# Sums of exponentials in the last chunk of an image attention: adds by VectorE and GpSimd in place of products with ones

## The chip, the cores and the metric

One core of one Trainium2 chip runs the whole program. The time is device microseconds of one execution; before the change the median of three runs is 12066.05 us (12055.0 to 12073.83). A matrix product runs on TensorE (PE in the profile), elementwise work on VectorE (DVE), ScalarE (ACT) and GpSimd (POOL). Each engine works through its own list of instructions in order; semaphores tie the lists together.

## The reference, cut to what matters

Four images of 56 x 56 points with 128 channels go through four layers. The first and the last layer are the same block: a window attention, then an attention over the whole image, then an MLP. The change lies in the attention over the whole image, so it is executed eight times (two layers, four images):

```python
def _mha(x, wq, bq, wk, bk, wv, bv, wo, bo):      # x: one image, 3136 points x 128 channels, 4 heads of 32
    ...
    scores = jnp.einsum('nhqd,nhkd->nhqk', q, k) / jnp.sqrt(jnp.float32(dk))
    attn = jax.nn.softmax(scores, axis=-1)
    out = jnp.einsum('nhqk,nhkd->nhqd', attn, v)
    ...
xf = xf + _mha(_layernorm(xf, g1, be1), wq, bq, wk, bk, wv, bv, wo, bo)
```

The softmax divides by the sum of exponentials over all 3136 keys. That sum, one number for each query and head, is what the change computes in another way.

## The kernel before

**Tiling.** The 3136 queries are cut into NCK = 7 chunks of CH = 448, the keys into NKB = 25 blocks of 128 (the last has 64). One step g of the loop (from L611) is one chunk and one block: qc is the chunk, k the block, g = 25 qc + k. Scores are made transposed, keys on the partitions and queries along the row, so a sum over keys runs partly over blocks (an add of whole tiles) and partly over the 128 partitions (a product with ones).

**One step on TensorE.** For each of four heads, `shifted` (L543) puts minus the row maximum into a PSUM bank, `score` (L552) adds keys times queries; ScalarE then writes the exponentials (L553) into a tile `e` that holds two heads, 128 x 896. `p = 0` is the pair of heads 0 and 1, `p = 1` heads 2 and 3; in an even step pair 0 comes first, in an odd step pair 1. At the end of the step `values(g - 1)` (L579) multiplies the values with the exponentials of the step before and gathers in the bank `po` over the whole chunk. PSUM banks of the tag "mm" go round in a ring of 7 (L500), tiles `e` in a ring of 12 (L551), that is six steps.

**The sum over the keys** has two ways. In `summed` (L555 to L563) GpSimd adds the tile `e` of block k onto a running tile `es`, one instruction for each pair of heads. Where k is in `by_ones(qc)` (L538) that add is left out, and `values` instead multiplies four heads by a matrix of ones into a bank `pd` (L568, called at L582), which ScalarE copies to `rest` the first time (L585) and VectorE adds to it afterwards (L587). In chunks 0 to 5 the blocks 4, 8, ... 24 go by ones (6 of 25), in the last chunk the blocks 4, 6, ... 24 (11 of 25). When a chunk is over, `total` (L594) multiplies `es` by ones into the bank `pt` (L568 too) and VectorE adds `rest` (L597); ScalarE inverts it by a logarithm and an exponential (`invert`, L602 and L604), GpSimd multiplies (L608).

**Order around it.** All is emitted in the order of the loop, by hand. `total(qc - 1)` comes at the end of step k = 4 of the next chunk, the two halves of `invert(qc - 1)` at the start of steps 5 and 6, ahead of the exponentials of these steps on ScalarE. The last chunk has no next one: its `total`, `invert` and product follow directly after its last `values`. Then the MLP begins, whose banks take the PSUM space of the loop (first product L683).

**Other work in the loop.** While chunks 0 to 5 run, TensorE and VectorE also find the row maxima of later queries (L371, L376). In the last chunk no maxima are left.

Of the kernel before, what the change touches and what calls it, by code (L numbers as in the profile page):

```python
# [10 lines left out]
F32 = mybir.dt.float32  # L11
# [3 lines left out]
ALU = mybir.AluOpType  # L15
# [4 lines left out]
P = 128  # L20
HW = 56
L = HW * HW
CH = 448
NCK = L // CH
# [10 lines left out]
NKB = (L + KB - 1) // KB  # L35
# [43 lines left out]
class _Net:  # L79
# [249 lines left out]
    def attention(self, layer, b, x1, oT, sb):  # L329
# [9 lines left out]
        nc, tc, w, x = self.nc, self.tc, self.w[layer], self.x_of(b)  # L339
# [23 lines left out]
        with tc.manual_schedule():  # L363
# [134 lines left out]
            with tc.tile_pool(name="at_sb", bufs=2) as tb, tc.tile_pool(name="at_ps", bufs=2, space=PSUM) as ps:  # L498
# [36 lines left out]

                made, es, sums = {}, {}, {}

                by_ones = lambda qc: range(4, NKB, 4) if qc < NCK - 1 else range(4, NKB, 2)  # L538
                pst = {}

                def shifted(g, h):
# [13 lines left out]
                def summed(g, p):  # L555
                    qc, k = divmod(g, NKB)
                    nk = min(KB, L - k * KB)
                    if k == 0:
                        if qc not in sums:
                            sums[qc] = tb.tile([P, NH, CH], F32, tag="es", name="es")  # L560
                    elif k not in by_ones(qc):
                        s = sums[qc][:nk, 2 * p : 2 * p + 2, :]
                        nc.gpsimd.tensor_tensor(s, es[g - 1, p][:nk] if k == 1 else s, es[g, p][:nk], ALU.add)  # L563

                def ones(n, src, into):

                    for h in range(NH):
                        nc.tensor.matmul(into[head(h), :CH], lhsT=self.one32[:n], rhs=src(h)[:n], start=True, stop=True)  # L568
# [25 lines left out]
                def total(qc):  # L594
                    pd = bank("pt")
                    ones(P, lambda h: sums[qc][:, h, :], pd)
                    nc.vector.tensor_add(made[qc]["rest"], pd[:, :CH], made[qc]["rest"])  # L597

                def invert(qc, step):
                    r = made[qc]["rest"]  # L600
# [10 lines left out]
                for g in range(ng + 8):  # L611
                    qc, k = divmod(g, NKB)
# [4 lines left out]
                    p = g % 2  # L617
# [4 lines left out]
                    if g < ng:  # L622


                        maxima(early_max, True)
                        maxima(late_max, False)
                        for h in first:
                            shifted(g, h)
                        for h in first:
                            score(g, h)  # L630
                        summed(g, p)
                    if g < ng:
                        shifted(g, early_max)
                        score(g, early_max)
                        shifted(g, late_max)
                        maxima(first[0], False)
                        score(g, late_max)
                        maxima(first[1], False)
                        summed(g, 1 - p)
# [3 lines left out]
                    if qc >= 1 and k == 4:  # L643
                        total(qc - 1)
# [991 lines left out]
```

## Time and profile before

The profiled execution took 12079.11 us, with a span of 12077.3 us from its first to its last instruction; the median of the runs is 12066.05 us. A table of what matters here, from the page and from windows of the trace:

| | first six chunks, first attention | last chunk, first attention | whole span |
|---|---|---|---|
| stretch, us from the start | 191.7 to 670.2 | 670.2 to 733.9 | 0 to 12077.3 |
| length, us | 478.5 | 63.7 | 12077.3 |
| TensorE busy, us | 476.7 | 63.1 | 10924.2 |
| VectorE busy, us | 368.8 | 8.1 | 9398.6 |
| ScalarE busy, us | 294.1 | 48.6 | 7556.4 |
| GpSimd busy, us | 450.7 | 55.1 | 9397.2 |

A busy TensorE is not one at its peak: its products are pipelined and up to four small ones run side by side, so their own durations add up to more than the busy time. In a group's line of the profile stand the source line, the engine, the operation, its output and inputs with their shapes, the count, the busy time, the mean length of one instruction in ns, and then the idle time of the engine just before these instructions with what ended it. In a timeline the first two numbers are the start in us and the length in us of a run of equal instructions.

### The profile page before, as it was taken

The page shows a single profiled execution, that of the slowest core. Times are in us where ns is not written, and L with a number is a line of the kernel's source. Part 1 is how long each engine was busy: PE and PEld are TensorE (multiplying, and loading weights), DVE is VectorE, ACT ScalarE, POOL GpSimd, SP SyncE. Part 2 cuts the span into 40 slices and gives each one's busy share as a digit, 9 for nine tenths or more (in the row PEclk, how much of TensorE's full clock was granted, in tenths as well). Part 3 has the DMA queues.
Part 4 walks back from the last instruction along what each step waited for, and adds up shares of the span by engine and source line. Part 5 has one row for each costly group of instructions (what it writes and reads, how often), then busy time and mean ns, then how long its engine had stood idle before and what let it go on. Part 6 is the DMA issues. An engine that isn't in the chain of part 4 may idle for free.

```text
span 12077.3 us, 219818 instructions
## 1 busy us (share of the span) xinstructions
PE 10924.2 (90%) x86844; PEld 7150.1 (59%) x86844; DVE 9398.6 (78%) x12051; ACT 7556.4 (63%) x19327; POOL 9397.2 (78%) x5876
## 2 busy tenths in 40 slices
PE   8998998997899899999889989999988998997799
PEld 5538885544688755454468865545446886553454
DVE  6749996767999877475899977747589997775674
ACT  5677776564677656656467765665646776564366
POOL 4949995795799759488689975948868997596497
PEclk9999999998899999999989999999989999998899
DMA  1000000005100000000610000000051000004200
GB/s 66 2 14 6 5 5 1 1 1 169 54 6 5 2 1 1 12 1 5 175 45 5 5 2 1 2 12 1 13 174 38 5 5 2 1 1 143 69 2 7
DMA packets 146295, 321.10 MB, mean 27 GB/s; under 512 B 17980, under 2 KB 87664, under 8 KB 145136
## 3 DMA queue, kind: packets, MB, share of 16 engines
q0 software_dynamic: 70848, 231.27, 6.6%
q1 hardware_dynamic: 74128, 74.57, 2.0%
q8 instruction: 687, 11.26, 0.4%
q14 instruction: 344, 2.82, 0.1%
q10 hardware_dynamic: 288, 1.19, 0.0%
HBM read 259.05 MB, written 47.90 MB: 25 GB/s over the span
## 4 chain that ended last, share of the span: by engine, by line
PE 59%; DVE 16%; POOL 11%; ACT 9%; issue 4%; DMA 1%; DVEq 0%; POOLq 0%; ACTq 0%; SPq 0%
PE pm L371 15%; PE po L579 10%; DVE hs L1126 9%; POOL hs L1135 9%; PE pst L552 7%; PE pst L543 3%; PE pd L568 2%; PE yt L1144 2%; PE pyb L1165 2%; PE dbu L1108 2%; PE pvt L1460 2%; DVE dgb L1012 1%; PE pdo L1468 1%; DVE mx L376 1%; ACT da L1063 1%
## 5 line engine op out<-in xcount | busy, mean ns | idle before, releaser
L376 DVE TENSOR_REDUCE mx<-pm 128x1 f32<-128x512 f32 (+7 forms) x6424 | 3377.5, 560 | 999.9 <-PE pm L371 924.1
L563 POOL TENSOR_TENSOR es<-es,e 128x896 f32<-128x896 f32 x1824 | 3764.1, 2090 | 77.1 <-ACT e L553 29.1
L1126 DVE TENSOR_TENSOR_SCAN hs<-da,dbu 128x928 f32<-128x928 f32 x1792 | 3617.4, 2068 | 31.9 <-ACT dbu L1119 16.1
L553 ACT ACTIVATE e<-pst 128x448 f32<-128x448 f32 (+1 forms) x5600 | 2592.0, 548 | 1530.3 <-PE pst L552 1076.3
L1135 POOL TENSOR_TENSOR hs<-hs,cb 128x896 f32<-128x896 f32 x1792 | 3434.8, 1950 | 16.4 <-ACT carry L1130 14.5
L371 PE MATMUL pm<-ks,qs 32*128 32x448 f32 (+5 forms) x12848 | 2963.9, 528 | 13.4 <-DVE nm L397 7.8
L552 PE MATMUL pst<-qs,ks 32*128 32x448 f32 x11200 | 2324.2, 539 | 0.0
L371 PEld LDWEIGHTS pm<-ks,qs 32*128 32x128 f32 x12848 | 1281.3, 187 | 1119.3 <-DVE mx L376 621.6
L1144 PE MATMUL yt<-w_C,hs 128*116 128x128 f32 x14336 | 1877.6, 274 | 16.2 <-POOL hs L1135 14.3
L543 PE MATMUL pst<-nm,sel 32*128 32x448 f32 x5600 | 1666.4, 527 | 6.9 <-DVE nm L397 6.9
L1144 PEld LDWEIGHTS yt<-w_C,hs 128*116 128x116 f32 x14336 | 1567.8, 136 | 42.2 <-POOL hs L1135 31.8
L1108 PE MATMUL dbu<-dgb,ut 112*128 112x224 f32 x7168 | 1248.7, 296 | 202.3 <-DVE hs L1126 199.4
L579 PE MATMUL po<-e,va 128*32 128x448 f32 (+1 forms) x11200 | 1358.6, 554 | 0.0
L1335 POOL DMA_INDIRECT g<-tab,idx x900 | 870.2, 967 | 505.9 <-issue 203.8
L552 PEld LDWEIGHTS pst<-qs,ks 32*128 32x128 f32 x11200 | 1253.9, 187 | 1.4
L1063 ACT ACTIVATE da<-dl,A 128x112 f32<-128x112 f32 x3584 | 1193.9, 382 | 0.1
L1108 PEld LDWEIGHTS dbu<-dgb,ut 112*128 112x128 f32 x7168 | 946.5, 192 | 323.4 <-DVE hs L1126 311.4
L543 PEld LDWEIGHTS pst<-nm,sel 32*128 32x128 f32 x5600 | 710.5, 185 | 164.3 <-issue 145.5
L1130 ACT COPY carry<-hs 128x32 f32<-128x32 f32 x1792 | 396.3, 221 | 551.0 <-DVE hs L1126 530.6
L297 POOL TENSOR_TENSOR pz<-s,m 64x784 f32<-64x784 f32 x128 | 191.8, 1498 | 681.2 <-DVE m L294 676.7
L579 PEld LDWEIGHTS po<-e,va 128*32 128x32 f32 (+1 forms) x11200 | 222.5, 108 | 824.8 <-issue 762.8
L1080 PE MATMUL pt<-w_C,dh 128*112 128x128 f32 x3584 | 551.7, 278 | 152.4 <-DVE dgb L1012 146.2
(227 smaller groups left out, 14365.6 us busy)
## 6 DMA issues: line engine op xcount, KB each, us to landing
g<-tab,idx POOLq DMA_INDIRECT x900, 3.7
tab<-zero SPq DMA_DIRECT2D x4, 3364.0 KB
dl_d<-dl SPq DMA_DIRECT2D x28, 448.0 KB
dl<-dl_d SPq DMA_DIRECT2D x56, 224.0 KB
tab<-gt SPq DMA_DIRECT2D x16, 448.0 KB
out_dram<-x SPq DMA_DIRECT2D x28, 224.0 KB
tab<-gt SPq DMA_DIRECT2D x16, 336.0 KB
x<-in_x_dram SPq DMA_DIRECT2D x21, 224.0 KB
```

The source lines that it names most:

```text
L371: nc.tensor.matmul(pm[:, at : at + m], lhsT=qs[head(h), q : q + P], rhs=ks[head(h), keys], start=True, stop=True)
L376: nc.vector.tensor_reduce(mx[:, i, h, n : n + 1], p, AX.X, ALU.max)
L543: nc.tensor.matmul(pst[g, h][:, :CH], lhsT=self.sel[head(h), :], rhs=nm[head(h), part(g // NKB)], start=True, stop=False)
L552: nc.tensor.matmul(t[:, :CH], lhsT=ks[head(h), k * KB : (k + 1) * KB], rhs=qs[head(h), part(qc)], start=False, stop=True)
L553: nc.scalar.activation(es[g, p][:nk, j, :], t[:nk, :CH], AF.Exp, scale=SCALE)
L563: nc.gpsimd.tensor_tensor(s, es[g - 1, p][:nk] if k == 1 else s, es[g, p][:nk], ALU.add)
L579: nc.tensor.matmul(m["po"][head(h), :CH], lhsT=va[:nk, k, head(h)], rhs=src(h)[:nk], start=(k == 0), stop=(k == NKB - 1))
L1063: nc.scalar.activation(m["da"][:, :, n, 2:], dl(), AF.Exp, scale=A[:, j, n : n + 1])
L1108: nc.tensor.matmul(pu[:, 8 * h : 8 * h + 8, 2 + tb * TB : 2 + (tb + 1) * TB], lhsT=made[g]["ut", 2 * r + tb][:, d, :], rhs=made["r", g // ...
L1126: nc.vector.tensor_tensor_scan(flat(pairs[u // 2][:, d % 2]), flat(made[g]["da"][:, r]), flat(banks.pop(u)), 0.0, ALU.mult, ALU.add)
L1135: nc.gpsimd.tensor_tensor(hs, hs, made["r", g // 2]["cb"][:, :, r * HW : (r + 1) * HW], ALU.mult)
L1144: nc.tensor.matmul(sums[q][:YR, e * P : (e + 1) * P], lhsT=hs[:, n, :], rhs=self.ident, start=(n == 0), stop=(n == NST // 2 - 1), is_trans ...
```

## The change

In the last chunk `by_ones` becomes empty, so every block is added elementwise there. The adds of the last chunk are dealt out: pair 0 always to VectorE; pair 1 to VectorE in odd blocks and to GpSimd in even blocks. In the other chunks GpSimd does all of them as before. Since in the last chunk no tile `rest` exists when `total` is reached, `total` makes it with a copy from `pt`.

```diff
-                by_ones = lambda qc: range(4, NKB, 4) if qc < NCK - 1 else range(4, NKB, 2)
+                by_ones = lambda qc: range(4, NKB, 4) if qc < NCK - 1 else ()
...
                     elif k not in by_ones(qc):
                         s = sums[qc][:nk, 2 * p : 2 * p + 2, :]
-                        nc.gpsimd.tensor_tensor(s, es[g - 1, p][:nk] if k == 1 else s, es[g, p][:nk], ALU.add)
+                        on = nc.vector if qc == NCK - 1 and (p == 0 or k % 2) else nc.gpsimd
+                        on.tensor_tensor(s, es[g - 1, p][:nk] if k == 1 else s, es[g, p][:nk], ALU.add)
...
                     ones(P, lambda h: sums[qc][:, h, :], pd)
-                    nc.vector.tensor_add(made[qc]["rest"], pd[:, :CH], made[qc]["rest"])
+                    if "rest" in made[qc]:
+                        nc.vector.tensor_add(made[qc]["rest"], pd[:, :CH], made[qc]["rest"])
+                    else:
+                        made[qc]["rest"] = tb.tile([P, CH], F32, tag="rest", name="rest")
+                        nc.vector.tensor_copy(made[qc]["rest"], pd[:, :CH])
```

## The prediction

> **What bounds the kernel now.** I read the chain of waits first (who sets the end), then windows over the eight last chunks (which engine is full there), then the timeline of single steps (what a round of ones costs), then the groups by shape.
>
> ```profile
> PE 59%; DVE 16%; POOL 11%; ACT 9%; issue 4%; DMA 1%; DVEq 0%; POOLq 0%; ACTq 0%; SPq 0%
> ...
> L878 DVE TENSOR_TENSOR sp_u<-sp_u,sp_e 128x896 f32<-128x896 f32 x28 | 30.5, 1088 | 23.5 <-ACT sp_u L874 23.5
> ...
> 670.00:731.00 61.00, 61.00 (x596) 20.08 (x596) 6.87 (x11) 48.11 (x104) 55.04 (x28) 1.00 0.01 2
> 5654.00:5718.00 64.00, 64.00 (x592) 20.85 (x588) 6.87 (x11) 47.72 (x104) 53.77 (x27) 0.94 0.01 1
> ```
>
> The window columns are length, then busy time of PE, weight loads, DVE, ACT and POOL, the granted clock, DMA. TensorE has no gap in the last chunk, VectorE works 6.87 us of 61, GpSimd 55, ScalarE 48. So TensorE paces it, and whatever leaves TensorE there counts until another engine is slower. Five of the eight last chunks are about 3.7 us longer (64.1 against 60.4 us from first to last exponential) at a granted clock of 0.94; the halved clock lies at their start (5651.9 to 5662.1 us in this one), before the first round of ones, so the rounds cost the same in all eight.
>
> ```profile
> 672.87 0.96 PE L579 MATMUL po<-e,va 128*32 128x448 f32 x8
> ...
> 674.93 0.96 PE L579 MATMUL po<-e,va 128*32 128x448 f32 x8
> ...
> 699.36 0.96 PE L579 MATMUL po<-e,va 128*32 128x448 f32 x8
> ...
> 701.42 0.96 PE L579 MATMUL po<-e,va 128*32 128x448 f32 x8
> ...
> 702.20 0.93 PE L568 MATMUL pd<-e,all 128*32 128x448 f32 x8
> ...
> 704.24 0.96 PE L579 MATMUL po<-e,va 128*32 128x448 f32 x8
> ```
>
> From one product with the values to the next is one step. Without a round of ones it is 2.06 us (674.93 - 672.87, and 701.42 - 699.36), with one 2.82 (704.24 - 701.42). Two steps: 4.88 now, 4.13 without (2 x 2.065). A round costs 0.75 us.
>
> **The change, part by part**
>
> *Rounds removed.* Eleven rounds in each of eight attentions. Ten (blocks 4 to 22) lie in the paced loop: 10 x 0.75 = 7.5 us each. The eleventh (block 24) lies in the tail and is counted there. What goes with them, one copy on ScalarE (0.56 us) and ten adds L587 on VectorE (0.625), is off the path, as are the 14 of 26 adds that leave GpSimd.
>
> *Adds on VectorE.* 36 in each last chunk, 128x896 from SBUF to SBUF; the last of each pair has 64 partitions. The same shape takes 1.09 us at L878. Bounds: 0.95 (128x768, L1449) and 2.09 (the GpSimd add itself). I take 1.09, as it is the same shape on the same engine. Two steps hold three VectorE adds and one GpSimd add: 3.27 and 2.09 us, both under 4.13. VectorE would pace only with adds over 1.38 (4.13 / 3). ScalarE needs 1.85 per step (four exponentials), under 2.065. So the 7.5 us are had, if the adds of the two engines run side by side.
>
> *Do they?* The trace has other pairs of this kind: deform's adds and products on VectorE with two SBUF inputs (L1447 to L1449) beside GpSimd's add of two SBUF tensors (L690).
>
> ```profile
> 2813.65 1.14 POOL L690 TENSOR_TENSOR x<-x,x 128x448 f32<-128x448 f32 x1 [3.47 <-DVE g L1448]
> 2813.67 0.95 DVE L1449 TENSOR_TENSOR g<-g,wt 128x768 f32<-128x768 f32 x1
> ```
>
> L690 takes 1.13 us at the median, L1449 0.953 (longest 0.955 of 300); overlapped for 0.95 us, both take just that. There are 31 such overlaps at L1447 to L1449, the same in each. An operation of another kind shows that the engines can get in each other's way: L162 (tensor_scalar, 0.51 us) takes 1.43 beside L690. I take no lengthening for the adds, with full exclusion as the other bound (rival D).
>
> The Trainium skill speaks against this change: "SBUF — State Buffer", section "Who interferes with whom", says that a VectorE instruction with two SBUF inputs contends with a GpSimd instruction that reads SBUF, and that the second one waits for the whole of the first. By it two steps would need 3.27 + 2.09 = 5.36 us, more than the 4.88 of now, and the kernel would become slower; by the rows at L1449 and L690 they need 4.13. I go by the rows.
>
> *VectorE's order: a new lateness at step 5.* Total(5), the add L597 for the chunk before, now stands behind the adds of steps 1 to 4 in VectorE's list, and one of them waits for GpSimd. First attention, times of now:
>
> ```profile
> 679.21 1.86 ACT L553 ACTIVATE e<-pst 128x448 f32<-128x448 f32 x4 [0.22 <-PE pst L552]
> ...
> 680.85 0.62 DVE L597 TENSOR_TENSOR rest<-pt,rest 128x448 f32<-128x448 f32 x1 [8.40 <-PE pt L568]
> 681.51 0.58 ACT L602 ACTIVATE rest<-rest 128x448 f32<-128x448 f32 x1 [0.44 <-DVE rest L597]
> ```
>
> GpSimd's add of block 2, pair 1, can start when the exponentials of step 2 end (676.93) and ends at 679.1. VectorE's add of block 3, pair 1, waits for it: 679.16 to 680.25. Behind it, block 3 and block 4 of pair 0: to 681.37 and 682.49. Then L597: 682.52 to 683.14, where it ends at 681.47 now. L602 is first in ScalarE's list of step 5, so the four exponentials behind it begin at 683.73, not 682.02, and end at 685.6. TensorE then stands: the values of step 5 wait for these exponentials until 685.66, where the shortened pace gives 683.95 (681.88 + 2.065). That is 1.7 us late; the second half of the inversion (L604, about 0.6 us of ScalarE at step 6, with 0.2 us of slack in a step) makes it 2.05. TensorE is the pacer, so it never gets this back. Lower bound 0.4 us (L597 as early as now, the two ScalarE instructions alone); upper bound with adds of 1.38: three of them behind the wait, 0.87 more, 2.9 us.
>
> *The tail.* Now the last exponential ends at 730.61 and L597 at 733.94, 3.33 us later; L683 of the MLP waits for that. After: GpSimd's add of block 24, pair 1, starts 0.07 us after the last exponential and takes 2.09 (64 partitions save nothing: L1447 takes 948 ns with 64 and 957 with 128); VectorE's last add ends by 1.44 and covers the first half. TensorE's products L568 then begin at 2.25 and take 0.96, VectorE's copy 0.07 + 0.62 (as L597; bounds 0.51 of L162 and 0.625): 3.9 us. 0.55 us lost each time, no matter that the eleventh round is gone; bounds 0.4 and 0.7.
>
> *Steady state.* VectorE's odd add of pair 1 waits each time for the GpSimd add that began with the end of the step before; it starts 2.15 us later, so VectorE stays about one step behind ScalarE (idle 0.86 us in 4.13). Behind it wait the adds of pair 0 only, and for these the tiles `e`, which have six steps of room: nothing.
>
> *Sum.* 7.5 - 2.05 - 0.55 = 4.9 us an attention, 39 us for eight. The profiled execution took 12079.1 us, 13 over the median; 12079 - 39 = 12040, against the median 12066 - 39 = **12027 us**. With the bounds: 8 x (7.5 - 2.9 - 0.7) = 31 and 8 x (7.5 - 0.4 - 0.4) = 54, and 10 us of scatter: 12010 to 12043.
>
> **Rivals**
>
> *B, no lateness at step 5.* If the adds of the first steps run earlier than I lay them out, 8 x (7.5 - 0.4 - 0.5) = 53 us: 12013. Against it: VectorE takes its list in order, and the wait for GpSimd's 2.09 us add stands ahead of L597.
>
> *C, the adds stretch each other in part.* With half of GpSimd's time lost to VectorE, two steps need 3.27 + 1.05 = 4.32: 12 x 0.19 = 2.3 us less, 2.6 us an attention, 21 in all: 12045, which the measurement hardly tells from no change. For it speaks L162's lengthening, against it the 31 undisturbed overlaps.
>
> *D, full exclusion of VectorE's and GpSimd's adds in the last chunk.* 36 x 1.09 + 12 x 2.09 + 1.15 (L608) = 65.5 us, from the first add at 674.06 to 739.6, then products and copy, 1.6: 741.2 against 733.94, 7.3 us an attention, 58 in all: 12124, slower. It decides from where the excluded share of GpSimd's time passes 0.41 (4.13 - 3.27 over 2.09), and eats the gain at about 0.6.
>
> *E, the change does not do what it says.* The order of instructions of the two programs excludes it: 352 products with ones are gone, and VectorE has the 36 adds per attention, L597's successor behind the seventh.
>
> **How the numbers follow.** Forecast 0.62, B 0.08, C 0.12, D and other losses 0.18. A measurement of this kernel tells about 0.2% (24 us) from no change, so faster is below 12042, slower above 12090: forecast and B are faster, 0.70; C is the same, 0.12; D is slower, 0.18. The range runs from 12006 (B less 7 us of scatter) to 12085: it takes in C and the way to D, and leaves out about 0.16 of D above and 0.03 below. The likeliest case alone has 12010 to 12043.
>
> **What would show it.** In the profile after: steps of 2.06 us between products with the values all through the last chunk from step 8 on; adds on VectorE of 1.09 us and on GpSimd of 2.09 while they overlap; L602's successor at step 5 some 1.7 us later after the exponentials of step 4 than now; last exponential to the copy 3.9 us; last chunks about 55 us from first to last exponential where they were 60.4. Adds longer than 1.4 us, or never overlapping, would show D. A pace above 2.1 us with short adds would mean that a wait I have not seen, ScalarE's for tiles `e` or for banks, has taken the place of the rounds.

## The result and the profile after

The changed kernel takes 12127.64 us (median of 5 runs, 12107.78 to 12134.96), the kernel before 12073.22 us in the same comparison: a ratio of 1.0045 [1.0034, 1.0056]. It is slower, where 12027 us was forecast; rival D, full exclusion of the two engines' adds, gave 12124. The profiled execution has a span of 12133.2 us, 55.9 more than before.

I read the second attention of each profile: in neither does its last chunk begin at a halved clock, as most others do (see the last section). First a window over its last chunk, from the first exponential to the end of the add or copy that makes the sum (length, then busy time of PE, weight loads, DVE, ACT and POOL, the granted clock, DMA share and GB/s), of the kernel before:

```profile
2651.20:2715.00 63.80, 63.05 (x608) 20.31 (x600) 8.12 (x13) 48.65 (x106) 55.06 (x28) 1.00 0.01 2
```

and of the changed kernel:

```profile
2658.60:2728.20 69.60, 59.55 (x520) 18.93 (x520) 55.62 (x39) 48.04 (x105) 33.62 (x14) 0.92 0.00 1
```

The chunk is 5.8 us longer. TensorE is no longer full; VectorE and GpSimd together are busy 89 us in 69.6. The view of the source line of the adds in the changed kernel (L564; shortest, median and longest in ns) says what became of single adds:

```profile
L564 POOL TENSOR_TENSOR es<-es,e x1728: 2071/2091/2919, 201.1 to 12060.9; 128x896 f32<-128x896 f32 x192
...
L564 DVE TENSOR_TENSOR es<-es,e x272: 1076/1084/2829, 681.6 to 12061.8; 128x896 f32<-128x896 f32 x136
```

The median is what I counted on, 1.08 and 2.09 us. The longest is 2.83 on VectorE and 2.92 on GpSimd, 1.75 and 0.83 us over these medians: most of one add of the other engine. The groups of a stretch in the middle of that last chunk (2680 to 2710 us; count, busy time, mean in ns):

```profile
L564 DVE TENSOR_TENSOR es<-es,e 128x896 f32<-128x896 f32 x18 | 28.2, 1610 | 4.6 <-POOL es L564 4.0
...
L564 POOL TENSOR_TENSOR es<-es,e 128x896 f32<-128x896 f32 x7 | 19.1, 2732 | 18.0 <-ACT e L553 13.8 <-DVE es L564 4.2
```

28.2 and 19.1 us of adds "at work" in 30 us of time cannot be free of each other when the same 18 and 7 adds would take 19.5 and 14.6 us alone. The time ends up at two places. One is step 5, in the timeline of the changed kernel:

```profile
2667.83 5.00 DVE L564 TENSOR_TENSOR es<-es,e 128x896 f32<-128x896 f32 x3 [1.99 <-POOL es L564]
...
2669.60 2.27 POOL L564 TENSOR_TENSOR es<-es,e 128x896 f32<-128x896 f32 x1 [1.81 <-ACT e L553]
...
2672.74 0.61 DVE L599 TENSOR_TENSOR rest<-pt,rest 128x448 f32<-128x448 f32 x1
2673.39 0.58 ACT L607 ACTIVATE rest<-rest 128x448 f32<-128x448 f32 x1 [3.86 <-DVE rest L599]
2673.41 0.46 PE L543 MATMUL pst<-nm,sel 32*128 32x448 f32 x1 [0.95 <-DVE rest L599]
```

Three adds take 5.00 us, since the third meets GpSimd's. L599 ends 3.83 us after the exponentials of step 4 (2669.52), where L597 ended 0.41 us after them; ScalarE waits 3.86 us for it, and TensorE for its bank. The other place is the tail, in the timeline of the changed kernel:

```profile
2714.64 1.83 ACT L553 ACTIVATE e<-pst 64x448 f32<-64x448 f32 x4 [0.22 <-PE pst L552]
...
2721.96 2.79 POOL L564 TENSOR_TENSOR es<-es,e 64x896 f32<-64x896 f32 x1 [2.09 <-DVE es L564]
2725.74 1.72 PE L569 MATMUL pt<-es,all 128*32 128x448 f32 x8 [8.29 <-DVE es L564]
2727.53 0.62 DVE L602 COPY rest<-pt 128x448 f32<-128x448 f32 x1 [1.84 <-PE pt L569]
```

and of the kernel before:

```profile
2709.79 1.82 ACT L553 ACTIVATE e<-pst 64x448 f32<-64x448 f32 x4 [0.96 <-PE pst L552]
...
2714.32 0.62 DVE L597 TENSOR_TENSOR rest<-pt,rest 128x448 f32<-128x448 f32 x1 [0.28 <-PE pt L568]
```

The last exponential is at 2716.47 and 2711.61, the end of the sum at 2728.15 and 2714.94: the tail has grown from 3.33 to 11.69 us. The adds are behind by the time ScalarE is done: VectorE's last ends at 2725.70 (ten adds, 17.48 us from 2708.22 on), and TensorE waits 8.29 us for it.

### The profile page after: what moved, and what is told of

It is laid out like the page before. It is cut to its first block, busy times and chain, and to the rows that moved or that the text cites. A ratio compares the mean times of both kernels' runs of the same rounds, so it can differ in the third digit from the quotient of the medians.

```text
span 12133.2 us, 218579 instructions
## 1 busy us (share of the span) xinstructions
PE 10897.5 (90%) x86140; PEld 7138.6 (59%) x86140; DVE 9780.9 (81%) x12259; ACT 7551.5 (62%) x19319; POOL 9229.9 (76%) x5764
## 4 chain that ended last, share of the span: by engine, by line
PE 58%; DVE 17%; POOL 11%; ACT 9%; issue 5%; DMA 1%; DVEq 0%; SPq 0%; ACTq 0%; POOLq 0%
PE pm L371 15%; PE po L580 10%; DVE hs L1131 9%; POOL hs L1140 8%; PE pst L552 7%; PE pst L543 3%; PE yt L1149 2%; PE pd L569 2%; PE dbu L1113 2%; PE pyb L1170 2%; PE pvt L1465 1%; DVE dgb L1017 1%; DVE mx L376 1%; ACT da L1068 1%; PE pdo L1473 1%
## 5 line engine op out<-in xcount | busy, mean ns | idle before, releaser
L564 POOL TENSOR_TENSOR es<-es,e 128x896 f32<-128x896 f32 x1728 | 3622.3, 2121 | 346.5 <-ACT e L553 213.9
L1140 POOL TENSOR_TENSOR hs<-hs,cb 128x896 f32<-128x896 f32 x1792 | 3436.1, 1948 | 19.7 <-ACT carry L1135 17.5
```

Source lines behind the costliest of these rows:

```text
L564: on.tensor_tensor(s, es[g - 1, p][:nk] if k == 1 else s, es[g, p][:nk], ALU.add)
L1140: nc.gpsimd.tensor_tensor(hs, hs, made["r", g // 2]["cb"][:, :, r * HW : (r + 1) * HW], ALU.mult)
```

## The experiments

Two explanations of the long adds were set against each other. The exclusion theory says that while one of the two engines works on an add of two SBUF tensors, the other's waits; the chain theory says that the long adds are waits for each other's partial sums in `es`.

**Adds alone.** The program leaves out the whole network and writes its input as its output; it runs eight VectorE operations beside four GpSimd adds, each engine on its own tiles. In short:

```diff
+nc.gpsimd.tensor_tensor(pa, pa, pb, ALU.add)      # x4, 896 or 448 columns
+nc.vector.tensor_tensor(va, va, vb, ALU.add)      # x8, several shapes; once with an input in PSUM
```

> Only adds, none of the network: eight adds on VectorE beside four on GpSimd, in eleven pairs of shapes, on tiles that nothing else touches. Exclusion theory: VectorE's 128x896 add of two SBUF tensors beside GpSimd's of the same shape gives stretched adds of 2.8 us and more on one of them, and the whole pair takes the sum of both alone, about 8 x 1.0 + 4 x 2.0 = 16 us; with one input in PSUM nothing is stretched, 8.4 us on both. Chain theory (the long adds of the changed kernel were waits for each other's partial sums): no stretching here, since no tile is shared; VectorE 1.09 and GpSimd 2.09 each. Open is which of the two the pair in deform's shape (256 x 3 beside 448) follows: in the kernel before it was never stretched.

Its timeline; the first two lines are each engine alone, then come three of the nine pairs: 128x896 on both, the shape of the prediction's deform rows (3 x 256 columns, here all in SBUF) beside 448 columns, and VectorE with one input in PSUM (`pv`).

```profile
56.43 8.96 DVE L48 TENSOR_TENSOR va<-va,vb 128x896 f32<-128x896 f32 x8
...
66.51 8.51 POOL L63 TENSOR_TENSOR pa<-pa,pb 128x896 f32<-128x896 f32 x4
...
75.33 10.70 POOL L63 TENSOR_TENSOR pa<-pa,pb 128x896 f32<-128x896 f32 x4 [0.19 <-ACT va L43]
75.83 15.66 DVE L48 TENSOR_TENSOR va<-va,vb 128x896 f32<-128x896 f32 x8
...
160.44 6.53 POOL L63 TENSOR_TENSOR pa<-pa,pb 128x448 f32<-128x448 f32 x4
160.91 10.84 DVE L54 TENSOR_TENSOR va<-va,vb 128x768 f32<-128x768 f32 x8
...
184.99 8.54 POOL L63 TENSOR_TENSOR pa<-pa,pb 128x896 f32<-128x896 f32 x4
185.45 8.96 DVE L57 TENSOR_TENSOR vc<-pv,vb 128x896 f32<-128x896 f32 x8
```

Alone 8.96 and 8.51 us; together 75.33 to 91.49, 16.2 us, not far from the sum of 17.5. While both work, VectorE's add takes 2.84 us and GpSimd's 2.80, as the source lines show (shortest, median and longest in ns):

```profile
L48 DVE TENSOR_TENSOR va<-va,vb x48: 957/1093/2844, 56.4 to 183.1; 128x896 f32<-128x896 f32 x40, 128x768 f32<-128x768 f32 x8
...
L63 POOL TENSOR_TENSOR pa<-pa,pb x40: 1125/2076/2802, 66.5 to 202.8; 128x896 f32<-128x896 f32 x32, 128x448 f32<-128x448 f32 x8
```

No tile is shared, so the chain theory has no ground here. With an input of VectorE in PSUM each keeps its time alone, 8.96 and 8.54; both still write to SBUF there, so it is the second read from SBUF that makes the difference. The pairs that are not shown all have two SBUF inputs on VectorE, and all are stretched (15.7 us for 896 columns, 10.84 for 768). And deform's shape is stretched as well (10.84 us, where its last four adds, beside nothing, take 0.957 us each) when all its operands lie in SBUF.

**Own sums.** GpSimd's even blocks of pair 1 go into a tile of their own (shortened; the first add of each tile is left out here):

```diff
+if k == 2: own["sum"] = tb.tile([P, 2, CH], F32, tag="es2", name="es2", bufs=1)
+t = s if k % 2 else own["sum"][:nk]
+on.tensor_tensor(t, t, es[g, p][:nk], ALU.add)
...
+nc.tensor.matmul(pd[head(h), :CH], lhsT=self.one32, rhs=own["sum"][:, h - 2, :], start=False, stop=True)
```

> The change with the same dealing of adds, but GpSimd gathers its blocks of pair 1 in a tile of its own, so that neither engine waits for the other's partial sum; total adds two products. Exclusion theory: the adds still stretch to 2.8 us, two steps still need 4.9 us, the time stays near the changed kernel's, 12110 to 12140 us. Chain theory: adds of 1.09 and 2.09 us, two steps in 4.13, about 12030 us.

12146.6 us (one run), somewhat above what exclusion expected and far from the chain theory's 12030. Groups from 690 to 725 us, in its first attention:

```profile
L576 DVE TENSOR_TENSOR es<-es,e 128x896 f32<-128x896 f32 x13 | 24.1, 1857 | 0.6
L574 POOL TENSOR_TENSOR es<-es,e 128x896 f32<-128x896 f32 x8 | 19.1, 2392 | 13.1 <-ACT e L553 13.1
```

No add waits for the other engine's partial sum any more (VectorE's idle time before them is 0.6 us), and they are still long. The waits for each other's partial sums are not the cause.

**No adds on GpSimd in the last chunk.** This leaves the even blocks of heads 2 and 3 out of the sum:

```diff
+if qc < NCK - 1 or on is nc.vector:
     on.tensor_tensor(s, es[g - 1, p][:nk] if k == 1 else s, es[g, p][:nk], ALU.add)
```

> The change without GpSimd's twelve adds in the last chunk: the even blocks of heads 2 and 3 are left out of the sum there. What is left is my forecast's sum without the two engines meeting. Exclusion theory: the 36 adds on VectorE take 1.09 us each, steps of 2.06 us, L599 about 0.6 us late, tail 2.6 us after the last exponential where before has 3.33: 8 x (7.5 - 1.0 + 0.7) = 58 us under before, 12010 to 12025 us. If VectorE's adds or its order were the loss, it stays over 12060.

12010.35 us, ratio 0.9958 [0.9943, 0.9972]. The tail is 2.64 us in all eight attentions and L599's successor ends 0.92 us after the exponentials of step 4, 0.5 later than in the kernel before. Groups from 690 to 720 us:

```profile
L565 DVE TENSOR_TENSOR es<-es,e 128x896 f32<-128x896 f32 x22 | 23.4, 1090 | 7.6 <-ACT e L553 6.9
```

The same 36 adds of VectorE, in the same order, at 1.09 us. So the rest of the forecast's sum (rounds, pace, VectorE's own load) holds; what it lacked sits in the meeting of the two engines. This is the cleanest evidence inside the kernel, though it takes GpSimd's work away as well as the meeting.

**All adds on VectorE**, and the same with total(5) at step 1:

```diff
-on = nc.vector if qc == NCK - 1 and (p == 0 or k % 2) else nc.gpsimd
+on = nc.vector if qc == NCK - 1 else nc.gpsimd
```

> All 48 adds of the last chunk on VectorE, none on GpSimd there. Exclusion theory: nothing is left to exclude; VectorE starts an add each 1.0 us, four in two steps are 4.0 against TensorE's 4.13, so steps of 2.06 us, no backlog at the end, total(5) about a microsecond late: 8 x (7.5 - 1.3 + 0.4) = 53 us under before, about 12015 us. Theory that VectorE is simply too slow for these adds: with 48 in place of 36 it becomes worse than the changed kernel, over 12130.

```diff
-if qc >= 1 and k == 4:
+if qc >= 1 and k == (1 if qc == NCK - 1 else 4):
     total(qc - 1)
```

> As the all-VectorE version, and total(5) is emitted at step 1 of the last chunk, ahead of the adds. If the lateness at step 5 is real, this takes another 0.5 to 1.5 us an attention away, 4 to 12 us in all, about 12005 us; if not, the same as the all-VectorE version.

12070.52 us, 0.9996 [0.9987, 1.0006], and 12050.09 us, 0.9977 [0.9968, 0.9987]. Against the changed kernel the first gains clearly, against the forecast of 12015 it misses. The step on TensorE is 2.07 us, as expected, but VectorE's 48 adds take 53.0 us and 55.3 to 56.8 from first to last, over 1.1 us each. The 1.0 us of the expectation was wrong: in the adds alone, too, eight take 8.96 us, 1.12 each. VectorE falls behind by some 0.3 us in two steps, and the tail is 6.7 to 7.3 us. The early total brought about 20 us where 4 to 12 were expected. From the first exponential of an attention to its sum it takes 1.0 to 1.4 us away (on average from 539.84 to 538.81 us where the last chunk does not begin at a halved clock, from 544.85 to 543.49 where it does), 8 to 11 us over eight; what makes up the rest of the 20 is not shown.

**The change with an early total(5)** (the second edit above, on the changed kernel):

> The change, with total(5) emitted at step 1 of the last chunk, ahead of the adds. Theory one, exclusion sets the end: the last add ends some 64 us after the first whatever ScalarE and TensorE do in between, so the last chunk ends sooner and its tail grows by as much; the time stays within 10 us of the changed kernel, about 12120 us. Theory two, the lateness at step 5 (3.2 us now) is the loss: it vanishes, some 3 to 5 us an attention, 12090 to 12100 us.

12095.83 us, 1.0026 [1.0017, 1.0035]. Neither theory is right by itself. By its number, theory two fits, but the kernel stays slower than before, and the tail grows from 11.7 to 14.05 us as theory one had it. The trace gives the shares: the time in which at least one of the two engines works on an add of the last chunk stays, 60.6 us before this edit and 60.2 after, in every attention; from the first add to the last it falls from about 64 to 61 or 62, since VectorE no longer idles around L599 and the stall it caused. From the first exponential of the attention to the sum the second attention goes from 547.7 to 545.9 us, and attentions whose last chunk begins at a halved clock from 552.4 to 550.4: 2 us, some 15 in eight, are the lateness. In the profiles three fewer last chunks begin at a halved clock, which is another 14 us of the 44.7 between them. What makes up the rest, and how the 23 us between the two ratios divide, is not shown.

**Two and three blocks by ones** on the early all-VectorE version:

```diff
-by_ones = lambda qc: range(4, NKB, 4) if qc < NCK - 1 else ()
+by_ones = lambda qc: range(4, NKB, 4) if qc < NCK - 1 else (12, 24)
```

> All adds of the last chunk on VectorE, total(5) early, and blocks 12 and 24 by ones, so that VectorE (1.1 us an add, four in two steps, 0.3 us more than TensorE's 4.14) has no backlog at the end. Exclusion theory with the add's measured pace: last chunk 0.75 us longer than in the early all-VectorE version, tail 3.3 in place of 7.2 us: 8 x (7.1 - 0.75) = 51 us under before, about 12020 us. If the backlog of VectorE is not what makes the tail, the tail stays at 7 us and the time is above that version's.

> As the version with two blocks by ones, with blocks 8, 16 and 24. One more round of 0.75 us: 8 x 0.75 = 6 us above it if two suffice against the backlog; below it if they do not.

12019.98 us, 0.9964 [0.9952, 0.9976], and with blocks 8, 16 and 24 12038.37 us, 0.9978 [0.9969, 0.9987]. Two rounds empty the backlog: the tail is 3.33 us in all attentions, as in the kernel before, and a third round only costs: 18 us where 6 were expected. In like attentions the third round costs 0.8 us (541.2 against 540.4 from the first exponential to the sum), the expected 6 in eight; in its profile all eight last chunks begin at a halved clock, six with two rounds, which is 9 us more. Both beat the kernel before and the change; the first is the fastest complete version of this study. The tail in its first attention, where VectorE now waits for TensorE again:

```profile
724.58 0.62 DVE L588 TENSOR_TENSOR rest<-pd,rest 128x448 f32<-128x448 f32 x1 [1.50 <-PE pd L569]
725.42 0.62 DVE L599 TENSOR_TENSOR rest<-pt,rest 128x448 f32<-128x448 f32 x1 [0.21 <-PE pt L569]
```

## Why the prediction was wrong

**The step that failed** is "Do they?", with its sentence "I take no lengthening for the adds, with full exclusion as the other bound (rival D)". The 31 overlaps at L1447 to L1449 were real, but those instructions do not have two SBUF inputs. The tile `wt` that holds the weights and the half products is in PSUM:

```python
with tc.tile_pool(name="df", bufs=1, side="right") as s1, tc.tile_pool(name="df_ps", bufs=1, space=PSUM, side="right") as s1x:
    ...
    far2 = s1x.tile([P, 2, 512], F32, tag="wt", name="wt").rearrange("q a b -> q (a b)")
```

A group's line names tiles and shapes, not their memory, and I called `g` and `wt` two SBUF inputs from the line alone. The adds alone show both sides of it: deform's shape with all operands in SBUF is stretched, a VectorE operation with one input in PSUM is not. The page that I weighed against these rows, "SBUF — State Buffer", section "Who interferes with whom" of the Trainium skill, says that a VectorE instruction with two SBUF inputs and a GpSimd instruction that reads SBUF exclude each other for the whole instruction, and that with at most one SBUF input outside the two-port modes nothing contends. The runs agree on both counts (2.84 and 2.80 us against 1.09 and 2.07; 8.96 and 8.54 us unchanged), and so did the rows I quoted against it. Only "the whole instruction" is a little too much: 16.2 us in place of 17.5 for four GpSimd adds beside eight of VectorE leave 0.33 us of each GpSimd add free, and in the last chunk of the changed kernel the adds take 60.6 us together where 36 x 1.09 + 12 x 2.09 = 64.3, 0.31 us for each of twelve.

**Point by point.** *Rounds removed*: right. Steps 8 to 22 run at 4.138 us for two (4.13 forecast, 4.88 before), in the changed kernel too: six steps of room in the tiles `e` let VectorE fall behind without holding TensorE. *VectorE's add*: right alone (1.08 to 1.09). *Lateness at step 5*: right in mechanism, too small: L599 ends 3.4 us later against the exponentials of step 4 than L597 did, not 1.7, because the adds ahead of it were stretched; in the second attention the last chunk's exponentials take 57.8 us where 55.0 was forecast (60.4 - 7.5 + 2.05). About half of these 2.9 us is something the prediction did not have: TensorE's clock falls to half for 3.41 us after this wait, and steps 6 and 7 take 5.5 us where the all-VectorE version, without that fall, takes 4.0. *Tail*: 11.69 us where 3.9 was forecast; this is where the backlog is paid. *Steady state*: wrong, VectorE does not stay one step behind: its last add ends 9.2 us after the last exponential. *Sum*: for the second attention +2.9 at step 5 and +7.8 in the tail on a forecast of -4.9 gives +5.8, the difference of the two windows. *Rival D*: its mechanism was right; that its 12124 lies so near 12127.64 is in part luck. It had 65.5 us of adds without a pause (with 1.15 for L608); from the first add to the last 63.1 to 64.2 were measured, 60.6 of them adds and the rest pauses. It charged 7.3 us an attention, 58 in all; measured are 5.4 in attentions whose last chunk does not begin at a halved clock and 5.6 in those where it does, some 44 in all, and 9 more come from two more such chunks in the profile after. Its chance of 0.18 rested on rows that did not bear on it. *The sum without the meeting*: the run without GpSimd's adds lies 56 us under before, more than the forecast's 39, since the lateness is then 0.5 us in place of 1.7 and the tail 2.64 in place of 3.9.

## What to carry to other kernels

Before a profile row is taken as evidence that two engines do not meet, look up in the code which memory each operand of both instructions lies in; the row's shape alone does not say it. Work taken from a full engine and dealt out to VectorE and GpSimd together counts as one engine's load where both read two tiles from SBUF: add their times (here 6 to 8% too much: 64.3 against 60.6 us, 17.5 against 16.2), and compare the sum with the pace. A loop with deep buffers can hide such an overload to its end, so read the tail as well as the pace.

## What was not expected of the hardware

*A half clock in the last chunk comes and goes.* The stretch of half clock near the start of the last chunk, which lengthens it by some 3.6 us, fell into 5 of the 8 attentions in the profile before, 7 after the change, 4 with the change and an early total, 6 with two blocks by ones. With some 1 us ahead of the chunk this is 9 of the 55.9 us between the two profiles ((7 - 5) x 4.6). The traces show what sets which attention is hit. In each trace all stretches of half clock begin at points of one grid, a whole number of 3.413 us apart (to 0.02 us over 12 ms). At the turn to the last chunk TensorE has two short gaps, 0.91 and 0.86 us, in every attention. Where 1.34 us or more of this idle time fall between two neighbouring points of the grid, the stretch follows; where it is 1.33 or less, it does not: 53 and 19 of the 72 last chunks in nine traces, without an exception. "TensorE: Matmul & The Clock Gate" in the Trainium skill (section "What's actually happening") describes a free-running window of 3.4 us in which activity is judged; the grid agrees with it, and which attention is hit is a matter of alignment. So these 9 us are no price of the change.

*The wait at step 5 halves the clock too.* In the second attention of the changed kernel eight products with the keys take nearly twice their time soon after the wait:

```profile
2666.67 0.94 PE L552 MATMUL pst<-qs,ks 32*128 32x448 f32 x8
...
2677.18 1.72 PE L552 MATMUL pst<-qs,ks 32*128 32x448 f32 x8
```

The granted clock is one half from 2676.6 to 2680.1. All eight last chunks after the change have such a stretch of 3.41 us. With own sums five have it, those in which the add of total(5) ends 3.7 us after the exponentials of step 4; the three in which it ends after 1.8 do not. In the kernel before and in every other version of the kernel none has it. Idle time alone does not tell here: from 2673.2 to 2676.6, just ahead of the stretch, TensorE is busy for 3.10 of 3.40 us, with 14 products where the chunk otherwise has about 40.

*The clock also falls while TensorE waits in the tail*: after 8.29 us of idle time the eight products at L569 take 1.72 us at their next start, where they take 0.94 at step 4 of the same chunk.

*GpSimd and VectorE alternate one instruction each* when both have work queued (VectorE 2.84 us, GpSimd 2.80, again and again in the adds alone), so neither is favoured there.
